# Two layers on one core: five x tiles, a bias, a transpose and the expert counts change places

## The chip, the cores and the metric

The kernel runs on one core of one Trainium2 chip. The metric is the device time of one execution in microseconds, as the median of several runs; the runs of the kernel before spread from 1205.78 to 1206.19 us. Beside it there is one profiled execution, whose time line names every instruction of every engine: TensorE (PE), VectorE (DVE), ScalarE (ACT), GpSimd (POOL) and SyncE (SP), which here only issues DMAs.

## The reference, cut to what matters

The input x is 4 images of 16 x 16 positions with 1024 channels: 1024 rows (tokens) of 1024 numbers, all in float32.

```python
x = x + conv_attention(group_norm(x))            # layer 0
t = to_tokens(x)                                  # 4 batches of 256 tokens
t = t + attention(layer_norm(t))                  # layer 1: 16 heads, causal, then
                                                  #   y @ W_proj.T + b_proj
t = t + experts(layer_norm(t))                    # gate, threshold 0.1, 8 experts
```

The experts' part, which the counts belong to:

```python
gate_logits = softmax(x @ gate_w + gate_b)
selected = gate_logits >= 0.1
weights = gate_logits * selected / (their sum)
out = sum over e of weights[:, e] * (x @ expert_w[e] + expert_b[e])
```

## The kernel before

Rows are worked on in 8 tiles of 128; tile t = 2 b + i is half i of batch b. Large products are done by a seven-product scheme (Strassen's form): a product of 2 x 2 blocks takes seven block products and some sums of blocks on VectorE. `sums_of_A` makes the sums of the row blocks s1, s2, s4 and changes a21 in place.

**End of layer 0.** Each tile of x is finished, normalised for layer 1, given the output bias b_proj by GpSimd, and stored in memory as `x_rows`. For the last two tiles worked on (tiles 4 and 6) the bias isn't added there: they are stored without it.

**Attention.** The loop over d (0 to 17) is a pipeline over 16 double steps and a lag of 2. Each step makes query and key products (`project_qk`), scores (`scores`, line 842), exponentials on ScalarE, the division by the row sums on GpSimd (`scored`, L883), a way through memory that cuts the scores in quarters (one store L889 and four loads L893 for each half, all on SP), a transpose on VectorE (`turn_back`, which calls `turned`, L898) and the product with v (`values`, pa, L911). TensorE's `values_and_scores(d)` needs the transposes of `turn_back(d)`.

From d = 13 on the output projection begins between these steps. It adds to tiles of x that `load_x` brings back from `x_rows` (GpSimd's queue, L1053), into memory that the attention's sums have left. `project_out` does a tile half directly; `product_out(b, n, ...)` does product n of the seven for the pair of tiles 2b and 2b + 1 (matmuls L980, VectorE's additions L987 to L1000). `sum_of_weights(1..4)` (L952) makes the sums of the weight blocks, 128 x 2048 each. `row_sums_out(b)` makes the row sums of pair b. Pair 1 (tiles 2 and 3) is done in d = 15 to 17 and one product more behind the loop; pair 2 (tiles 4 and 5) and then tiles 6 and 7 follow in the part called the rest here. At d = 17 GpSimd adds the bias to tiles 4 and 6 (L1103), with a tile `bp` that is loaded at d = 15 (L1084).

**The rest: projection beside the gate.** While TensorE does the remaining projection, one finished tile after another goes through eight stages: 0 normalise (statistics L1258, root L141 to L143, row on ScalarE L170, through memory in quarters as L1276 and L182; the tile itself goes to the output, L1283), 1 turn the row (L187), 2 gate sums (`parts`, L1325), 3 gate (`pg`), 4 thresholds, 5 place (the products `pp`, L1382 and L1383, with the running counts `kept`, L1380), 6 entries and 7 lists. Stages 2 to 5 take tiles 0 to 2 together, then 3 to 5, then 6, then 7.

The order is written by hand. TensorE's matmuls of this part are counted (a chunk is one matmul of 128 x 128 by 128 x 512, 0.86 us in two passes), and the table `at_chunk` says behind which chunk which (stage, tile) is put; `others` does the same for single steps, among them `row_sums_out(2)` at chunk 12. Chunks 9 to 12 are the last product of pair 1, 13 to 40 the seven of pair 2 in the order 1, 2, 6, 7, 5, 3, 4, then 8 for each half of tiles 6 and 7. Parts of the program inside `manual_schedule` keep the written order on each engine; between two such parts, and for steps outside them (the gate's constants, say, L1206 to L1245), the framework's scheduler merges by the order of the text and by what is ready, so steps of the rest can stand ahead of the loop's last ones.

The rest's tiles come from pools that lie where the attention's tiles were; a tile there waits for the last reader of what it covers. Product banks: three called mm and three called tr; pair 2's products all take mm banks in turn, so a product waits until VectorE has taken up the one three before it.

**After it.** Eight experts follow, each with its gathered rows and products; that is the larger part of the second half.

Of the kernel before, what the change touches and what calls it, by code (L numbers as in the profile page):

```python
# [32 lines left out]
F32 = mybir.dt.float32  # L33
# [6 lines left out]
P = 128  # L40
C = 1024
# [4 lines left out]
NT = TOK // P  # L46
# [16 lines left out]
Q = 4  # L63
# [6 lines left out]
def kernel(  # L70
# [27 lines left out]
    nc = tc.nc  # L98

    def pool(stack, name, bufs=1, **kw):  # L100
        return stack.enter_context(tc.tile_pool(name=name, bufs=bufs, reuse_waits="tile", **kw))
# [121 lines left out]
            nc.scalar.copy(dst[:, 4 * j : 4 * j + 4, ts(t, P)], pt.rearrange("p (c n) -> p c n", c=4))  # L223


    in_order, bp_home = ExitStack(), ExitStack()
    with ExitStack() as layer0:
        l0 = pool(layer0, "l0")
        xn = x_pool.tile([P, NC, TOK], F32, tag="x", name="xn")
# [434 lines left out]
    with ExitStack() as attention:  # L664
# [295 lines left out]
        def row_sums_out(b):  # L960
            a, s = rows_out_of(b)
            sums_of_A(*a, *s)
# [64 lines left out]
        with tc.manual_schedule():  # L1027
            for d in range(len(doubles) + lag):
                if d % 4 == 0 and d < 12:
                    load_qk(d // 4 + 1)  # L1030
                elif d == 12:
                    w_p.append(w_tile("w_p0", W_projT[:, :HALF]))

                def values_and_scores(at):
                    if at >= lag:
                        values(at - lag, turned_s.pop(at - lag))
                    if at < len(doubles):
                        made[at] = scores(at)

                def go_on(at, between=lambda: None):  # L1040
                    if at - 1 in made:
                        first_one, second_one = made.pop(at - 1)
                        soft[at - 1] = [scored(*first_one)]
                        between()
                        soft[at - 1].append(scored(*second_one))

                def turn_back(at):
                    if at >= lag:
                        turned_s[at - lag] = [turned(*one) for one in soft.pop(at - lag)]

                def load_x(*some):
                    for t in some:
                        nc.gpsimd.dma_start(xs[t], x_rows[ts(t, P), :])  # L1053

                ahead = units.get(d, ())
                if d < 14:
                    for unit in ahead[:1]:
                        project_qk(*unit)
                    turn_back(d)
                    go_on(d)  # L1060
                    for unit in ahead[1:]:
                        project_qk(*unit)
                    if d == 13:
                        sums.close()
                        x_pool = pool(x_home, "xb", side="right")
                        xs = [x_pool.tile([P, C], F32, tag=f"x{t}", name=f"xb{t}") for t in range(NT)]
                        bp = pool(bp_home, "bp", side="right").tile([P, C], F32, tag="bp", name="bp")
                        load_x(0)
                    values_and_scores(d)
                elif d == 14:  # L1070
                    project_qk(*ahead[0])
                    go_on(14, lambda: load_x(1))
                    project_qk(*ahead[1])
                    turn_back(14)
                    w_p.append(w_tile("w_p1", W_projT[:, HALF:]))
                    sums_out.append(big_tile(1, "sums_out", (4 * Q, HALF)))
                    load_x(2)
                    project_out(*outs[14][0], {NC - 3: lambda: values_and_scores(14)}, True)
                    turn_back(15)
                    project_out(*outs[14][1], {}, True)  # L1080
                    go_on(15)
                    load_x(3)
                elif d == 15:
                    nc.gpsimd.dma_start(bp, b_proj.partition_broadcast(P))  # L1084
                    product_out(1, 1, tr)
                    product_out(1, 2, tr, {1: lambda: values_and_scores(15)})
                    sum_of_weights(1)
                    sum_of_weights(2)
                    project_out(*outs[15], {NC - 1: lambda: go_on(16)}, True)
                    row_sums_out(1)  # L1090
                    load_x(4, 6)
                    turn_back(16)
                elif d == 16:
                    project_out(*outs[16], {}, True)
                    load_x(5, 7)
                    product_out(1, 6, mm)
                    sum_of_weights(3)
                    product_out(1, 5, mm, {1: lambda: values_and_scores(16)})
                    sum_of_weights(4)
                    turn_back(17)  # L1100
                else:
                    for b, nt in tiles[NT - 2 :]:
                        nc.gpsimd.tensor_add(xs[2 * b + nt], xs[2 * b + nt], bp)  # L1103
                    product_out(1, 3, tr)
                    product_out(1, 7, tr, {1: lambda: values_and_scores(17)})
        share_banks("ps_rest", 3)
        bp_home.close()


    left.close()  # L1110
# [91 lines left out]
    with ExitStack() as gating:  # L1202
# [149 lines left out]
            nc.scalar.activation(weight, weight, AF.Exp)  # L1352
            return weight, top, keep

        def thresholds(weight, top, keep):
            n = top.shape[1]
            all_of = top.unsqueeze(2).to_broadcast([P, n, E])
            if n > 1:
                nc.vector.tensor_reduce(top, weight, AX.X, ALU.add)
            nc.vector.reciprocal(top, top)  # L1360
            if n == 1:
                of = weight[:, 0, :]
                nc.vector.tensor_scalar(keep[:, 0, :], of, top, THRESHOLD, ALU.mult, ALU.is_ge)
                nc.vector.scalar_tensor_tensor(of, of, top, keep[:, 0, :], ALU.mult, ALU.mult)
            else:
                nc.vector.tensor_mul(weight, weight, all_of)
                nc.vector.tensor_scalar(keep, weight, THRESHOLD, None, ALU.is_ge)
                nc.vector.tensor_mul(weight, weight, keep)
            nc.vector.tensor_reduce(top, weight, AX.X, ALU.add)
            nc.vector.scalar_tensor_tensor(top, top, 0.0, top, ALU.is_equal, ALU.add)  # L1370
            nc.vector.reciprocal(top, top)
            nc.vector.tensor_mul(weight, weight, all_of)
            return keep

        def place(tiles, keep):


            n, t0 = len(tiles), tiles[0]
            for i, t in enumerate(tiles):
                nc.vector.tensor_add(kept[:, t + 1, :], kept[:, t, :], keep[:, i, :])  # L1380
            pp = tr(f"pp{t0}")[:, : n * E]
            nc.tensor.matmul(pp, before, keep.rearrange("p n e -> p (n e)"), start=True, stop=False)  # L1382
            nc.tensor.matmul(  # L1383
                pp, ones, kept[:, t0 : t0 + n, :].rearrange("p n e -> p (n e)"), start=False, stop=True
            )
            slot = of_tiles("place", n, E)
            nc.vector.scalar_tensor_tensor(slot, keep, 0.0, from_end[:, t0 : t0 + n, :], ALU.is_equal, ALU.mult)
            at = l2w.tile([P, 3, n, E], I32, tag="at", name=f"at{t0}", padded_shape=[P, 3, 3, E])
            nc.vector.tensor_add(at[:, 0, :, :], slot, pp.rearrange("p (n e) -> p n e", n=n))
            nc.vector.tensor_scalar(at[:, 1, :, :], at[:, 0, :, :], 31, None, ALU.bitwise_and)  # L1390
            nc.vector.tensor_scalar(at[:, 2, :, :], at[:, 0, :, :], 5, None, ALU.logical_shift_right)
            return at
# [74 lines left out]
        def stage(n, t):  # L1467
            tiles = together[t]
            if n == 0:
                normal[t] = normalise(t)  # L1470
            elif n == 1:
                turned_rows[t] = turn_rows(t, normal[t])
            elif n == 2:
                summed[t] = gate_sums(tiles)
            elif n == 3:
                gated[t] = gate(tiles, summed[t])
            elif n == 4:
                gated[t] = thresholds(*gated[t])
            elif n == 5:
                placed[t] = place(tiles, gated[t])  # L1480
            elif n == 6:
                entered[t] = entries_of(t, t - tiles[0], placed[tiles[0]])
            else:
                enter(t, *entered[t])
# [16 lines left out]
            47: ((7, 1),),  # L1501
            48: ((1, 4),),
            50: ((7, 2),),
            53: ((1, 5),),
            55: ((2, 3),),
            57: ((0, 6),),
            58: ((3, 3),),
            59: ((4, 3),),
# [11 lines left out]
        def load_table(function):  # L1520

            of = small.tile([P, 1], F32, tag="first", name="first", bufs=1)
            nc.scalar.activation(of, ident[:, 0:1], function)

        others = {
            12: lambda: row_sums_out(2),
            29: lambda: nc.gpsimd.dma_start(
                w_p[1][:, : NC // 2, :], W_projT[:HALF, HALF:].rearrange("(c p) n -> p c n", p=P)
            ),
# [447 lines left out]
```

## Time and profile before

| | us |
|---|---|
| median of 3 runs | 1206.02 |
| lowest, highest | 1205.78, 1206.19 |
| the profiled execution | 1204.73 |
| its span, first to last instruction | 1202.9 |
| TensorE busy in the span | 1191.1 (99%) |
| VectorE busy | 799.0 (66%) |
| GpSimd busy | 416.2 (35%) |
| ScalarE busy | 211.2 (18%) |

Times in the views are microseconds from the span's start. A line of a timeline has start, length, engine, line of the program, operation, written tile <- read tiles, shape and count; in brackets stands how long the engine had been idle before it and what ended that. The granted clock of TensorE was 1.00 in all stages looked at here. In the time line, d = 15 runs from about 609 us, d = 17 from 641.7 us, chunk 9 of the rest from 652.2 us, pair 2 from 655.7 us, and the experts from about 740 us.

### The profile page before, as it was taken

The page shows a single profiled execution, that of the slowest core. Times are in us where ns is not written, and L with a number is a line of the kernel's source. Part 1 is how long each engine was busy: PE and PEld are TensorE (multiplying, and loading weights), DVE is VectorE, ACT ScalarE, POOL GpSimd, SP SyncE. Part 2 cuts the span into 40 slices and gives each one's busy share as a digit, 9 for nine tenths or more (in the row PEclk, how much of TensorE's full clock was granted, in tenths as well). Part 3 has the DMA queues.
Part 4 walks back from the last instruction along what each step waited for, and adds up shares of the span by engine and source line. Part 5 has one row for each costly group of instructions (what it writes and reads, how often), then busy time and mean ns, then how long its engine had stood idle before and what let it go on. Part 6 is the DMA issues. An engine that isn't in the chain of part 4 may idle for free.

```text
span 1202.9 us, 13637 instructions
## 1 busy us (share of the span) xinstructions
PE 1191.1 (99%) x4866; PEld 649.3 (54%) x4866; DVE 799.0 (66%) x1394; ACT 211.2 (18%) x523; POOL 416.2 (35%) x470
## 2 busy tenths in 40 slices
PE   9999999999999999999999999999999999999998
PEld 5444884788884444444544464454344435444544
DVE  5796736678332666566679867897677767667852
ACT  3310111130001222122221212111111111111111
POOL 1051351365000122222333116546474554555411
PEclk9999999999999999999999999999999999999999
DMA  9102014882201353535565777484757475666434
GB/s 348 35 1 70 19 41 112 273 277 69 70 9 62 102 174 109 163 93 167 164 199 181 228 245 242 101 234 113 223 121 220 100 241 130 189 145 198 77 62 72
DMA packets 94330, 170.83 MB, mean 142 GB/s; under 512 B 12048, under 2 KB 49440, under 8 KB 94256
## 3 DMA queue, kind: packets, MB, share of 16 engines
q1 hardware_dynamic: 72880, 105.08, 26.6%
q0 software_dynamic: 16960, 54.59, 19.1%
q10 hardware_dynamic: 4416, 10.22, 2.4%
q8 instruction: 40, 0.66, 0.2%
q14 instruction: 34, 0.28, 0.1%
HBM read 117.17 MB, written 48.50 MB: 138 GB/s over the span
## 4 chain that ended last, share of the span: by engine, by line
PE 93%; DVE 3%; DMA 2%; issue 1%; SPq 0%; ACT 0%; POOL 0%; DVEq 0%; POOLq 0%
PE p L1662 27%; PE pqk L682 15%; PE pv L682 8%; PE joint L1724 4%; PE pq_pair L413 4%; PE pq L328 4%; PE left L1769 3%; PE po L1006 3%; PE pT L525 3%; PE py L617 2%; PE pk L444 2%; PE pc L465 2%; PE pv L553 2%; PE sc L842 2%; PE rest L1783 2%; PE pa L911 2%
## 5 line engine op out<-in xcount | busy, mean ns | idle before, releaser
L1145 POOL DMA_INDIRECT w_e_xg<-rows,gather x146 | 164.3, 1125 | 54.2 <-issue 42.4
L1662 PE MATMUL p<-w_e,A 128*128 128x512 f32 x368 | 162.1, 593 | 0.0
L883 POOL TENSOR_TENSOR s_q<-s_q,total 128x128 f32<-128x128 f32 (+1 forms) x128 | 61.8, 518 | 275.3 <-DVE total L880 264.4
L1662 PEld LDWEIGHTS p<-w_e,A 128*128 128x128 f32 x368 | 69.6, 190 | 86.8 <-issue 85.9
L1168 POOL DMA_INDIRECT out_dram<-y,add x32 | 58.7, 1834 | 163.6 <-issue 78.6
L1662 PE MATMUL p<-T,S 128*128 128x512 f32 x256 | 112.7, 592 | 0.0
L1711 ACT ACTIVATE y<-y,slot 128x512 f32<-128x512 f32 x64 | 45.4, 721 | 318.1 <-DVE y L1676 146.6
L682 PE MATMUL pqk<-ln,w_qk 128*128 128x512 f32 x192 | 85.7, 595 | 0.0
L1662 PEld LDWEIGHTS p<-T,S 128*128 128x128 f32 x256 | 48.6, 190 | 60.8 <-issue 60.3
L868 ACT ACTIVATE s_q<-sc,top 128x128 f32<-128x128 f32 (+1 forms) x128 | 52.0, 419 | 156.4 <-DVE top L864 137.8
L682 PEld LDWEIGHTS pqk<-ln,w_qk 128*128 128x128 f32 x192 | 36.1, 190 | 43.7 <-issue 42.1
L682 PE MATMUL pqk<-T,S_qk 128*128 128x512 f32 x128 | 57.8, 595 | 0.0
L1662 PE MATMUL p<-w_e,S 128*128 128x512 f32 x128 | 57.5, 592 | 0.0
L1006 PE MATMUL po<-w_p,y_T 128*128 128x512 f32 x112 | 50.7, 599 | 0.0
L328 PE MATMUL pq<-w_q,xn 128*128 128x512 f32 x96 | 44.5, 599 | 0.3 <-ACT xn L308 0.3
L682 PE MATMUL pv<-w_v,ln 128*128 128x256 f32 x192 | 43.2, 379 | 0.0
L1769 PE MATMUL left<-w_e,one 128*32 128x512 f32 x312 | 41.8, 593 | 0.0
L1662 PEld LDWEIGHTS p<-w_e,S 128*128 128x128 f32 x128 | 24.3, 190 | 30.6 <-issue 28.9
L898 DVE STREAM_TRANSPOSE s_T<-s_rows 128x768 f32<-128x768 f32 x32 | 30.2, 962 | 15.9 <-DMA s_rows<-s_rows 15.7
L187 DVE STREAM_TRANSPOSE A<-w_e_xg 128x1024 f32<-128x1024 f32 x32 | 39.5, 1235 | 1.4 <-DMA w_e_xg<-rows,gather 1.3
L682 PEld LDWEIGHTS pqk<-T,S_qk 128*128 128x128 f32 x128 | 24.0, 190 | 29.2 <-issue 27.7
L682 PEld LDWEIGHTS pv<-w_v,ln 128*128 128x128 f32 x192 | 36.4, 190 | 4.9
(388 smaller groups left out, 2056.0 us busy)
## 6 DMA issues: line engine op xcount, KB each, us to landing
w_e<-in_expert_w_dram SPq DMA_DIRECT2D x13, 2048.0 KB, 11.4
s_rows<-s_q SPq DMA_DIRECT2D x32, 384.0 KB, 2.3
s_rows<-s_rows SPq DMA_DIRECT2D x128, 96.0 KB, 2.4
w_qk<-in_W_attnT_dram SPq DMA_DIRECT2D x8, 1024.0 KB, 5.7
w_e<-in_expert_w_dram ACTq DMA_DIRECT2D x3, 2048.0 KB, 11.2
w_q<-in_Wq_dram SPq DMA_DIRECT2D x16, 256.0 KB, 6.8
x_at<-in_x_dram POOLq DMA_DIRECT2D x8, 512.0 KB
w_p<-in_W_projT_dram SPq DMA_DIRECT2D x2, 2048.0 KB, 8.3
```

Source lines behind the costliest of these rows:

```text
L328: nc.tensor.matmul(pq, xn[:, c, ts(t, P)], w_q[kc][:, c, :], start=(c == 0), stop=(c == NC - 1))
L413: nc.tensor.matmul(bank, a[:, c, :], b[:, c, :], start=(c == 0), stop=(c == NC // 2 - 1))
L682: nc.tensor.matmul(bank, stationary(c), moving(c), start=(c == 0), stop=(c == NC // 2 - 1))
L868: nc.scalar.activation(blocks(h, qt), psc[:, h, cols].rearrange("p (b f i) -> p b f i", f=Q, i=32), AF.Exp, bias=top[:, qt, h : h + 1], sc ...
L883: nc.gpsimd.tensor_mul(blocks(h, qt), blocks(h, qt), total[:, qt, h : h + 1].unsqueeze(2).unsqueeze(3).to_broadcast([P, 1 + qt, Q, 32]),)
L1006: nc.tensor.matmul(po, y_T[:, c, ts(t, P)], w_p[j][:, c, :], start=(c == 0), stop=(c == NC - 1))
L1145: nc.gpsimd.indirect_dma_start(out=row[:, g, :], out_offset=None, in_=table[: (TOK - P) * Q, :] if e in SHORT else table, in_offset=bass.I ...
L1168: nc.gpsimd.indirect_dma_start(out=out[: TOK - P, :] if e in SHORT else out, out_offset=bass.IndirectOffsetOnAxis(ap=add[:slots, e, k : k ...
L1662: nc.tensor.matmul(bank, a[:, c, :], b[:, c, :], start=(c == 0), stop=(c == NC // 2 - 1))
L1711: nc.scalar.mul(y, y, slot[:, e, 1, k : k + 1])
L1724: nc.tensor.matmul(of, a[:, c, :], b[:, c, :], start=(c == 0), stop=(c == NC // 4 - 1))
L1769: nc.tensor.matmul(bank[ts(i, 32), :], stationary, w[of][j][:, c, :], start=(c == 0), stop=(c == NC - 1))
```

## The change

- The tile `bp` isn't a pool of its own any more and isn't loaded at d = 15. It is made ahead of the rest in the pool l2w, under the tag that the experts' bias uses later, and loaded there on GpSimd's queue.
- Tiles 4 and 6 get their bias (`add_bias`, GpSimd) at chunks 13 and 22 of the rest and no longer at d = 17.
- x tile 4 is loaded at the end of d = 14 with tile 3; tiles 5, 6 and 7 are loaded at d = 17 on SP's queue. Before, 4 and 6 were loaded at d = 15 and 5 and 7 at d = 16, on GpSimd's queue.
- `turn_back(17)` stands ahead of `sum_of_weights(4)`.
- The additions to `kept` move from stage 5 (place) to stage 4 (thresholds), each behind its tile's selection.
- The turn of tile 5 moves from chunk 53 to 54, the gate sums of tiles 3 to 5 from 55 to 56.
- `row_sums_out(2)` moves from chunk 12, behind tile 2's normalisation, to chunk 10, ahead of it.

```diff
@@ -223,7 +223,7 @@
             nc.scalar.copy(dst[:, 4 * j : 4 * j + 4, ts(t, P)], pt.rearrange("p (c n) -> p c n", c=4))
 
 
-    in_order, bp_home = ExitStack(), ExitStack()
+    in_order = ExitStack()
     with ExitStack() as layer0:
         l0 = pool(layer0, "l0")
         xn = x_pool.tile([P, NC, TOK], F32, tag="x", name="xn")
@@ -1064,7 +1064,6 @@
                         sums.close()
                         x_pool = pool(x_home, "xb", side="right")
                         xs = [x_pool.tile([P, C], F32, tag=f"x{t}", name=f"xb{t}") for t in range(NT)]
-                        bp = pool(bp_home, "bp", side="right").tile([P, C], F32, tag="bp", name="bp")
                         load_x(0)
                     values_and_scores(d)
                 elif d == 14:
@@ -1079,32 +1078,28 @@
                     turn_back(15)
                     project_out(*outs[14][1], {}, True)
                     go_on(15)
-                    load_x(3)
+                    load_x(3, 4)
                 elif d == 15:
-                    nc.gpsimd.dma_start(bp, b_proj.partition_broadcast(P))
                     product_out(1, 1, tr)
                     product_out(1, 2, tr, {1: lambda: values_and_scores(15)})
                     sum_of_weights(1)
                     sum_of_weights(2)
                     project_out(*outs[15], {NC - 1: lambda: go_on(16)}, True)
                     row_sums_out(1)
-                    load_x(4, 6)
                     turn_back(16)
                 elif d == 16:
                     project_out(*outs[16], {}, True)
-                    load_x(5, 7)
                     product_out(1, 6, mm)
                     sum_of_weights(3)
                     product_out(1, 5, mm, {1: lambda: values_and_scores(16)})
+                    turn_back(17)
                     sum_of_weights(4)
-                    turn_back(17)
                 else:
-                    for b, nt in tiles[NT - 2 :]:
-                        nc.gpsimd.tensor_add(xs[2 * b + nt], xs[2 * b + nt], bp)
+                    for t in (5, 6, 7):
+                        nc.sync.dma_start(xs[t], x_rows[ts(t, P), :])
                     product_out(1, 3, tr)
                     product_out(1, 7, tr, {1: lambda: values_and_scores(17)})
         share_banks("ps_rest", 3)
-        bp_home.close()
 
 
     left.close()
@@ -1352,8 +1347,8 @@
             nc.scalar.activation(weight, weight, AF.Exp)
             return weight, top, keep
 
-        def thresholds(weight, top, keep):
-            n = top.shape[1]
+        def thresholds(tiles, weight, top, keep):
+            n = len(tiles)
             all_of = top.unsqueeze(2).to_broadcast([P, n, E])
             if n > 1:
                 nc.vector.tensor_reduce(top, weight, AX.X, ALU.add)
@@ -1361,10 +1356,13 @@
             if n == 1:
                 of = weight[:, 0, :]
                 nc.vector.tensor_scalar(keep[:, 0, :], of, top, THRESHOLD, ALU.mult, ALU.is_ge)
+                nc.vector.tensor_add(kept[:, tiles[0] + 1, :], kept[:, tiles[0], :], keep[:, 0, :])
                 nc.vector.scalar_tensor_tensor(of, of, top, keep[:, 0, :], ALU.mult, ALU.mult)
             else:
                 nc.vector.tensor_mul(weight, weight, all_of)
                 nc.vector.tensor_scalar(keep, weight, THRESHOLD, None, ALU.is_ge)
+                for i, t in enumerate(tiles):
+                    nc.vector.tensor_add(kept[:, t + 1, :], kept[:, t, :], keep[:, i, :])
                 nc.vector.tensor_mul(weight, weight, keep)
             nc.vector.tensor_reduce(top, weight, AX.X, ALU.add)
             nc.vector.scalar_tensor_tensor(top, top, 0.0, top, ALU.is_equal, ALU.add)
@@ -1376,8 +1374,6 @@
 
 
             n, t0 = len(tiles), tiles[0]
-            for i, t in enumerate(tiles):
-                nc.vector.tensor_add(kept[:, t + 1, :], kept[:, t, :], keep[:, i, :])
             pp = tr(f"pp{t0}")[:, : n * E]
             nc.tensor.matmul(pp, before, keep.rearrange("p n e -> p (n e)"), start=True, stop=False)
             nc.tensor.matmul(
@@ -1475,7 +1471,7 @@
             elif n == 3:
                 gated[t] = gate(tiles, summed[t])
             elif n == 4:
-                gated[t] = thresholds(*gated[t])
+                gated[t] = thresholds(tiles, *gated[t])
             elif n == 5:
                 placed[t] = place(tiles, gated[t])
             elif n == 6:
@@ -1501,8 +1497,8 @@
             47: ((7, 1),),
             48: ((1, 4),),
             50: ((7, 2),),
-            53: ((1, 5),),
-            55: ((2, 3),),
+            54: ((1, 5),),
+            56: ((2, 3),),
             57: ((0, 6),),
             58: ((3, 3),),
             59: ((4, 3),),
@@ -1522,8 +1518,16 @@
             of = small.tile([P, 1], F32, tag="first", name="first", bufs=1)
             nc.scalar.activation(of, ident[:, 0:1], function)
 
+        bp = l2w.tile([P, Q, C // Q], F32, tag="bias", name="bp", bufs=1).rearrange("p a b -> p (a b)")
+        nc.gpsimd.dma_start(bp, b_proj.partition_broadcast(P))
+
+        def add_bias(t):
+            nc.gpsimd.tensor_add(xs[t], xs[t], bp)
+
         others = {
-            12: lambda: row_sums_out(2),
+            10: lambda: row_sums_out(2),
+            13: lambda: add_bias(4),
+            22: lambda: add_bias(6),
             29: lambda: nc.gpsimd.dma_start(
                 w_p[1][:, : NC // 2, :], W_projT[:HALF, HALF:].rearrange("(c p) n -> p c n", p=P)
             ),
```

## The prediction

> **What bounds the kernel now.** I read the page first: busy times and the chain of waits.
>
> ```profile
> PE 1191.1 (99%) x4866; PEld 649.3 (54%) x4866; DVE 799.0 (66%) x1394; ACT 211.2 (18%) x523; POOL 416.2 (35%) x470
> PE 93%; DVE 3%; DMA 2%; issue 1%; SPq 0%; ACT 0%; POOL 0%; DVEq 0%; POOLq 0%
> ```
>
> TensorE is the bound. The change neither adds nor removes a product, so it can only move TensorE's idle time: 1202.9 - 1191.1 = 11.8 us in the whole span. Everything the diff touches runs between about 585 and 735 us. So the next view is TensorE's waits in 590 to 740 us (what waited, for what, us, times, longest):
>
> ```profile
> PE pa L911 <- DVE s_T L898: 2.1, 2, 1.8
> PE pp L1383 <- DVE kept L1380: 1.0, 1, 1.0
> PE row_pt L1303 <- DVE row L1282: 0.5, 1, 0.5
> PE po L980 <- DVE xb L996: 0.2, 1, 0.2
> ```
>
> TensorE's timeline gives the places (start, length, idle time and releaser in brackets):
>
> ```profile
> 648.85 1.64 PE L911 MATMUL pa<-s_T,v 128*64 128x256 f32 x16 [1.85 <-DVE s_T L898]
> 662.92 3.70 PE L980 MATMUL po<-sums_out 128*128 128x512 f32 x8 [0.21 <-DVE xb L996]
> 683.79 0.40 PE L1383 MATMUL pp<-kept,ones 128*128 128x24 f32 x2 [0.98 <-DVE kept L1380]
> ```
>
> The edits aim at these three. Together they are 1.85 + 0.21 + 0.98 = 3.04 us, the most that can be won. A difference under 0.2% (2.4 us) is about what a measurement of this kernel cannot tell from no change, so even the full prize is only just visible.
>
> **Who makes TensorE late.** VectorE's timeline ahead of the first gap, then GpSimd's:
>
> ```profile
> 637.54 1.74 DVE L991 TENSOR_TENSOR xb<-xb,sums_out 128x512 f32<-128x512 f32 x1
> 639.20 4.43 DVE L952 TENSOR_TENSOR w_p<-w_p 128x2048 f32<-128x2048 f32 x1
> ...
> 645.54 2.28 DVE L952 TENSOR_TENSOR sums_out<-w_p,sums_out 128x2048 f32<-128x2048 f32 x1
> 647.74 1.82 DVE L898 STREAM_TRANSPOSE s_T<-s_rows 128x768 f32<-128x768 f32 x2
> ```
>
> ```profile
> 631.68 2.16 POOL L1053 DMA_DIRECT2D xb<-x_rows  x4
> 636.38 5.10 POOL L1103 TENSOR_TENSOR xb<-xb,bp 128x1024 f32<-128x1024 f32 x2 [2.55 <-DMA xb<-x_rows]
> ```
>
> The transposes that TensorE waits for (turn_back(17)) stand behind the fourth weight sum, 2.28 us. The third sum took 4.43 us where its like takes 2.28, and L991 took 1.74 where a 128x512 add takes 0.69: both ran while GpSimd added the bias (636.38 to 641.48). And the chain of waits shows that the scores' second half came late through memory anyway:
>
> ```profile
> 634.05 8.85 DMA s_rows<-s_q
> ...
> 644.28 2.49 DMA s_rows<-s_rows
> ```
>
> The first took 8.85 us, where the median of its line is 2.3, with the four x loads of 631.68 in flight. The second landed at 646.8, so at 647.0, when TensorE was ready, only the first transpose could have been done.
>
> **The change, part by part.**
>
> *turn_back(17) before the fourth sum.* VectorE is free for it at 645.54 or sooner. Even if the DMAs stayed as late as now, the first transpose ends at 646.5, the second (landing 646.8 + 0.97) at 647.8. The first eight products need only the first, so at most 0.1 us of the 1.85 remains. The fourth sum then ends by 650.1 at the latest; its user (L980 of the last product of pair 1) starts at 650.4 in the moved schedule. Gain 1.85.
>
> *The x tiles.* Tile 4 takes the place that the bias load had on GpSimd's queue (614.8), same size. Tiles 5, 6 and 7 go on SP behind the scores' five DMAs, so those find the DMA engines free at 634: 2.3 to 3.6 us for 8.85, landing near 641. This is cover for the first gain, worth nothing more by itself. Three more issues on SP (0.38 each) stand ahead of SP's later stores and quarter loads, which before began at 654.98. First use of these tiles is near 670, so nobody waits. [...]
>
> *The two bias additions.* Removing them at 636.38 gives VectorE back (1.74 - 0.69) + (4.43 - 2.28) = 3.2 us, all of it before 643.6, where TensorE did not wait. They come back on GpSimd behind the load of the bias. That tile is now the first of its pool, so I expect it where the last-read values v lie: its load waits for the last pa (near 648.5 now), behind the gate's fill, two loads and constants (2.5 us, as from 650.57 to 653.07 before), so issue near 651.5 and, by the 4.1 us that the first of the four x loads took (632.2 to 636.3), landing near 655. Adds from 655 to 660, 2.34 us each. First users: L989 on tile 4, which TensorE needs (its bank) at 664.4; tile 6 is used near 690. Slack 4 us and more.
>
> What they can hurt is VectorE at 655 to 660. The rows: an add of two operands in SBUF stretched by 1.05 and 2.15 us, while L987 at 636.81, with one operand in PSUM, kept its 0.69. Cost between 0 and, from these rows, 3.2 us (4.7 if VectorE stands still for both adds) on VectorE. [...]
>
> *Side effect of that tile.* If it is the pool's first, the first normalised row no longer lies over v. Before, ScalarE's first row stood idle for 18.12 us until the last pa (650.54), with its inputs ready at 634.3. It may now run at once, and with it the second row's root and its two small VectorE instructions. That takes about 0.3 us off VectorE after 650 and moves 3 MB of stores and loads into 636 to 650. I cost it at nothing; if it crowds the scores' DMAs, see the rival.
>
> *Row sums at chunk 10.* Same four instructions, 0.69 each = 2.8 us, now ahead of tile 2's normalisation, not behind it. Both stand before L996, which frees the bank that TensorE waited for at 662.92. So the order does not take work from before L996. It helps if the sums run in VectorE's idle time before the last pa; the scheduler already pulled tile 0's and 1's statistics forward like this (627.98, 634.25).
>
> *Counts with the thresholds.* Three adds, 0.53 us together, move from 683.40 to 678.5, so the second pp product finds them done: gain 0.98. Their new place delays the thresholds by 0.53, ahead of no waiting TensorE. The turn of tile 5 and the next gate sums move one chunk (0.86) later against TensorE, which comes 0.98 sooner there, while VectorE's chain is 0.5 shorter: even. Cost 0.
>
> **Where VectorE gives back.** With the first gap closed TensorE reaches the product of 662.92 at 662.71 - 1.85 = 660.86. VectorE must have ended L996. Before, from L998 at 649.50 to L996's end at 662.87 was 13.4 us with 0.9 idle. Now L998 starts near 647.3 (transposes 643.2 to 645.0, fourth sum to 647.3). The same work without the idle ends at 647.3 + 12.5 = 659.8, plus the collision: 0 to 4.7. If the row sums are pulled ahead of the constants, the adds meet about one two-operand instruction (L994), 1 to 2 us: end 660.8 to 661.8, wait 0 to 0.9. I take 0.4, near the low end, because L996 itself has an operand in PSUM.
>
> Sum: 3.04 - 0.4 = 2.6 us. The profiled execution took 1204.73 us (span 1202.9 and 1.8 around it), so 1202.1 by it; it was 1.3 below the median of the runs, and from the median 1206.02 - 2.6 = **1203.4**.
>
> **Rivals.**
> 1. *VectorE takes the gap over* (no change, chance 0.36): the sums are not pulled forward and meet the adds. L996 then ends at 662 to 663 and TensorE waits 1.1 to 2.1 at the same product; only 0.98 and a rest remain, 1203.6 to 1206. For it: VectorE was 5.34 of 6 us busy in 655 to 661. Against: the scheduler's pulling forward.
> 2. *Slower* (0.17): the same collision at its full 4.7 us. L996 ends at 664.5, TensorE waits 3.6; and tile 2's normalisation, now behind the sums, ends 4 us later than at 659.61. Its row goes through memory (ACT row 659.65, transpose 670.65) and TensorE needs it within the gate sums, 1.0 us after 671.70. Its transpose would end near 676 for a need at 672.7, so net 3.04 - 0.2 - 3.3 - 2 = 2.5 us lost: 1208.5. It decides from about 3 us of collision on.
> 3. *The edits do not do what they say* (within the 0.36): SP's queue puts tile 0's stores and quarter loads ahead of the scores' last four DMAs, and these land at 649, not 646.8. Then 1.85 shrinks to nothing and 1205 remains.
>
> **Chances.** Forecast, the gaps closed and at most 0.6 us given back (1202.9 to 1203.6): 0.47, all of it faster by over 0.2%. Rivals 1 and 3, 0.36: within 0.2%. Rival 2, 0.17. The range runs from the full prize, 1203.0, with the 0.4 by which such runs differ, to the point where rival 2 begins to count: 1202.6 to 1207.3. The forecast alone: 1202.8 to 1203.7.
>
> **What would show it.** Right: no idle time before pa near 647; s_rows<-s_q near 3 us; L952's third sum at 2.3 us; pp without a wait; GpSimd's two adds near 655. Wrong: a wait of over 0.6 us on L996 or L989 at the sixth product of the second pair; row sums of 1.5 us and more each; the gate sums waiting for a transpose; pa still waiting for s_T. Outside 590 to 735 us nothing should differ.

## The result and the profile after

The changed kernel took 1210.34 us (median of 6 runs, 1209.05 to 1211.3), the kernel before 1205.68 (6 runs, 1204.89 to 1206.19): ratio 1.0038, 95% interval 1.0025 to 1.0051. It is slower, by about 4.7 us, and lies above the predicted range. The profiled execution took 1209.66 us with a span of 1207.9; before it was 1204.73 and 1202.9.

The page's busy times: TensorE still does the same 4866 matmuls; its busy time is 0.8 us more (1191.1 before) and the span 5.0.

```profile
span 1207.9 us, 13640 instructions
PE 1191.9 (99%) x4866; PEld 648.9 (54%) x4866; DVE 799.1 (66%) x1394; ACT 211.3 (17%) x523; POOL 416.0 (34%) x467
```

TensorE's waits between 590 and 745 us (what waited, for what, us in total, times, longest):

```profile
PE po L980 <- DVE xb L996: 5.1, 1, 5.1
PE parts L1320 <- DVE row_T L187: 0.9, 1, 0.9
PE row_pt L1298 <- DVE row L1277: 0.6, 1, 0.6
PE pa L911 <- DVE s_T L898: 0.4, 1, 0.4
```

The 0.4 on pa is an earlier one, at 598.42 us. The last pa near 647 and pp no longer wait. TensorE's timeline shows the same places as before:

```profile
646.93 1.52 PE L911 MATMUL pa<-s_T,v 128*64 128x256 f32 x16
...
665.76 5.09 PE L980 MATMUL po<-sums_out 128*128 128x512 f32 x8 [5.10 <-DVE xb L996]
...
677.90 0.65 PE L1320 MATMUL parts<-row_T,gw 128*32 128x128 f32 x16 [0.88 <-DVE row_T L187]
...
687.99 0.38 PE L1379 MATMUL pp<-kept,ones 128*128 128x24 f32 x2
```

Two gaps are closed, but the third, the sixth product of pair 2, has grown from 0.21 to 5.10 us. There is something else in its line: its eight passes took 5.09 us where they took 3.70 before. The table of windows shows why. Its columns are the window, its length, busy time of PE, PEld, DVE, ACT and POOL (instructions in brackets), then TensorE's granted clock, the DMA share and GB/s:

```profile
663.00:665.70 2.70, 0.00 (x0) 0.00 (x0) 2.33 (x8) 0.76 (x2) 0.00 (x0) 0.91 0.34 121
665.70:668.50 2.80, 2.73 (x4) 1.19 (x5) 2.19 (x4) 1.27 (x2) 0.00 (x0) 0.50 0.95 290
668.50:669.50 1.00, 1.00 (x4) 0.52 (x3) 0.96 (x3) 0.00 (x0) 0.00 (x0) 0.95 1.06 434
```

At the end of the long idle time the clock fell to half and stayed there for some 3 us of work. Around the 1.85 us gap of before it had stayed at 1.00.

VectorE's timeline tells who was late:

```profile
637.54 0.69 DVE L991 TENSOR_TENSOR xb<-xb,sums_out 128x512 f32<-128x512 f32 x1
638.15 2.28 DVE L952 TENSOR_TENSOR w_p<-w_p 128x2048 f32<-128x2048 f32 x1
...
643.10 1.83 DVE L898 STREAM_TRANSPOSE s_T<-s_rows 128x768 f32<-128x768 f32 x2
...
648.50 0.88 DVE L929 TENSOR_SCALAR y_T<-pa,bv 128x256 f32<-128x256 f32 x2 [0.81 <-PE pa L911]
650.41 0.69 DVE L987 TENSOR_TENSOR sums_out<-po,sums_out 128x512 f32<-128x512 f32 x1 [1.03 <-PE po L980]
...
654.56 5.06 DVE L1230 COPY copies<-ident 32x128 f32<-32x128 f32 x4
...
660.12 0.69 DVE L160 TENSOR_TENSOR sums_out<-y_T 128x512 f32<-128x512 f32 x1
...
665.03 0.68 DVE L996 TENSOR_TENSOR xb<-xb,po 128x512 f32<-128x512 f32 x1
```

The third weight sum and L991 are back at their plain lengths, as forecast. But four tiny copies of the gate's constants (L1230, the loop that fills `copies`) took 5.06 us. In GpSimd's timeline the two bias additions stand at the same time, and the chain of waits (start, length, what) takes the four copies apart: two of over 2 us, then, with the additions over, two of 0.22.

```profile
654.42 4.65 POOL L1525 TENSOR_TENSOR xb<-xb,bp 128x1024 f32<-128x1024 f32 x2 [2.92 <-DMA bp<-in_b_proj_dram]
```

```profile
654.64 2.20 DVE copies L1230
...
656.86 2.29 DVE copies L1230
...
659.16 0.22 DVE copies L1230
```

**Where the 4.3 us come from.** From 609 us, where the two traces coincide, to the experts' first products: -1.85 (pa) + 4.89 (L996's wait, 0.21 to 5.10) + 1.39 (half clock, 3.70 to 5.09) + 0.88 (gate sums) - 0.98 (pp) = +4.33. The experts begin 4.29 us later and the last line of products as much (1183.08 to 1187.37). The rest of the span's 5.0 arises behind it.

**The theory** to be tested: VectorE's copies (0.22 us alone, 2.20 and 2.29 here) and its sums of two operands from SBUF (L991 and L952 before, 1.74 and 4.43 us beside the additions, 0.69 and 2.28 here) stand still while a GpSimd addition runs. The change moved those additions from a stretch where TensorE did not wait to one where VectorE was already the last to come. The rival: VectorE is simply overfull before L996, by the row sums pulled ahead or by the transposes taken before the fourth sum, and the additions matter little.

### The profile page after: what moved, and what is told of

Its sections match the earlier page's. It is cut to its first block, busy times and chain, and to the rows that moved or that the text cites. A ratio compares the mean times of both kernels' runs of the same rounds, so it can differ in the third digit from the quotient of the medians.

```text
span 1207.9 us, 13640 instructions
## 1 busy us (share of the span) xinstructions
PE 1191.9 (99%) x4866; PEld 648.9 (54%) x4866; DVE 799.1 (66%) x1394; ACT 211.3 (17%) x523; POOL 416.0 (34%) x467
## 4 chain that ended last, share of the span: by engine, by line
PE 95%; DVE 2%; DMA 1%; SPq 0%; issue 0%; ACT 0%; DVEq 0%
PE p L1666 27%; PE pqk L682 16%; PE pv L682 8%; PE joint L1728 4%; PE pq_pair L413 4%; PE po L1006 4%; PE pq L328 3%; PE left L1773 3%; PE pT L525 3%; PE po L980 2%; PE py L617 2%; PE pk L444 2%; PE pc L465 2%; PE pv L553 2%; PE sc L842 2%; PE pa L911 2%
```

## The experiments

Twelve kernels, in three groups, each group on one chip beside the kernel before, whose medians there were 1204.84, 1204.84 and 1204.58 us; so ratios are compared. "From the change" and "from before" name the kernel that was edited.

### no_adds: the change without the additions

```diff
-            13: lambda: add_bias(4),
-            22: lambda: add_bias(6),
```

> The changed kernel without the two bias additions of chunks 13 and 22 (tiles 4 and 6 then lack the output bias; the bias is still loaded). Theory A (the additions on GpSimd, 654.4 to 659.1, hold VectorE's two copies of 2.2 us each, and these make L996 late): the copies at L1230 take 0.22 us each, L996 ends near 661.6, TensorE waits about 1.0 us at the sixth product of pair 2 and keeps its full clock there. Tile 2's row still goes to memory later than before the change, since the row sums stand ahead of it, so the gate sums wait for its transpose by up to 2 us. Time 1204.5 to 1206. Rival B (the row sums' place alone makes L996 late): the wait stays at 4 us or more, time above 1208.5. Rival C (tile 0's early loads and the x tiles on SP crowd something): no change, 1210.

1206.3 us, ratio 1.0006 (0.9997 to 1.0015). VectorE's copies, then TensorE:

```profile
655.09 0.89 DVE L1230 COPY copies<-ident 32x128 f32<-32x128 f32 x4
```

```profile
662.13 3.70 PE L980 MATMUL po<-sums_out 128*128 128x512 f32 x8 [0.93 <-DVE xb L996]
...
674.09 1.05 PE L1320 MATMUL parts<-row_T,gw 128*32 128x128 f32 x16 [2.10 <-DVE row_T L187]
675.07 3.22 PE L980 MATMUL po<-sums_out 128*128 128x512 f32 x4
```

The copies fall by 4.17 us (5.06 to 0.89) and the wait for L996 by the same 4.17 (5.10 to 0.93): at this product the additions act through these copies alone. But the gain does not come up: with TensorE no longer late, a second wait of 2.10 us appears at the gate sums, and after it the next products run slowly again (four passes in 3.22 us, 1.98 elsewhere). Theory A named that wait but not its slow clock, and the time is 0.3 us above the expected 1206.

### adds_in_loop and adds_loop_sums12: the additions at another time

Both from the change: bias and x tiles 4 and 6 are loaded at the end of d = 14, GpSimd adds at the head of d = 17. The second also puts the row sums back to chunk 12.

```diff
-                    load_x(3, 4)
+                    load_x(3, 4, 6)
+                    nc.gpsimd.dma_start(bp, b_proj.partition_broadcast(P))
...
-                    for t in (5, 6, 7):
+                    for t in (4, 6):
+                        nc.gpsimd.tensor_add(xs[t], xs[t], bp)
+                    for t in (5, 7):
...
# the second only
-            10: lambda: row_sums_out(2),
+            12: lambda: row_sums_out(2),
```

> The changed kernel with the bias part as it was in place, but earlier: bias and x tiles 4 and 6 loaded on GpSimd at the end of d = 14, the additions on GpSimd at the head of d = 17, so right behind the last divisions of the scores (from about 632 us); tiles 5 and 7 stay on SP. Theory A: the additions run from 632 to 637, where VectorE had idle time, the copies at L1230 take 0.22 us each, and the rest is as without additions: 1204.5 to 1206. Rival B: as the changed kernel, above 1208.5. Rival C: 1209 or more.

> As the kernel before it in this list, and row_sums_out(2) back at chunk 12, behind tile 2's normalisation. Theory A with the row sums as a second, smaller cost (tile 2's row 2.8 us later through memory): the wait at the sixth product stays near 1 us, no wait at the gate sums, and the gains of the other edits show: 1203 to 1204. If the row sums' place costs nothing, the same time as with them at chunk 10. Rival B: this one alone is fast, and by 4 us or more against the kernel with the sums at chunk 10.

adds_in_loop: 1206.5 us, ratio 1.0015 (1.0007 to 1.0024). adds_loop_sums12: 1202.63 us, ratio 0.9989 (0.998 to 0.9999), below the changed kernel and just below the kernel before; three of its twelve executions took 1205.4 to 1207.3, and no trace shows why. In adds_in_loop GpSimd adds from 630.70 to 635.81, a stretch where VectorE is not the last to come; the collision is there (a 128x1 instruction took 2.06 us) and TensorE does not feel it:

```profile
633.77 2.06 DVE L169 SCALAR_TENSOR_TENSOR ln_less<-ln_mv,ln_rstd 128x1 f32<-128x1 f32 x1
```

What remains of its loss is at the gate sums, in TensorE's timeline:

```profile
673.33 0.64 PE L1325 MATMUL parts<-row_T,gw 128*32 128x128 f32 x16 [2.19 <-DVE row_T L187]
673.90 3.65 PE L980 MATMUL po<-sums_out 128*128 128x512 f32 x4
```

With the row sums at chunk 12 this wait is gone, and so is the slow product behind it; the wait for L996 is the same (0.94, against 0.92):

```profile
661.50 3.70 PE L980 MATMUL po<-sums_out 128*128 128x512 f32 x8 [0.94 <-DVE xb L996]
...
670.28 1.52 PE L1325 MATMUL parts<-row_T,gw 128*32 128x128 f32 x48
671.72 1.98 PE L980 MATMUL po<-sums_out 128*128 128x512 f32 x4
```

The pair therefore prices the row sums' move: 2.19 of waiting and 3.65 - 1.98 = 1.67 of slow clock (granted 0.50 from 674 to 677), 3.86 us; the medians differ by 3.87, an agreement closer than medians with intervals of about 1 us to each side can vouch for. The move lets 2.8 us of VectorE work stand ahead of tile 2's statistics, and that tile's row goes through memory and back before TensorE's gate sums need it.

### counts_only and turn_only: single parts on the kernel before

counts_only takes the three edits of the counts (additions in `thresholds`, chunks 54 and 56) and nothing else. turn_only takes the exchange alone:

```diff
+                    turn_back(17)
                     sum_of_weights(4)
-                    turn_back(17)
```

> The kernel before with the counts' edit alone: additions to kept in the thresholds, turn of tile 5 at chunk 54, gate sums of tiles 3 to 5 at chunk 56. If the prediction's third term was right: no wait ahead of the second pp product, 1.0 us less, about 1204.7. If the moved chunks or the longer thresholds cost something: 1205.7 or more.

> The kernel before with one edit, the last transposes of the scores ahead of the fourth weight sum. Theory (VectorE is the bound after that point): the wait before pa falls from 1.85 us to at most 0.3, and the 6th product of pair 2 waits 1 to 2 us for L996 in its place (0.2 before), since VectorE's work up to L996 is the same; time within 1 us of the kernel before, 1204 to 1205. Rival (the gap is won for good): both waits gone, 1.8 us less, 1203.

counts_only: 1203.64 us, ratio 0.9987 (0.9979 to 0.9996). The wait of pp is gone; the waits of pa (1.62) and L996 (0.22) stay. The 0.98 us of the prediction is there. turn_only: 1203.74 us, ratio 0.9991 (0.9982 to 1.0), with these waits of TensorE:

```profile
PE po L980 <- DVE xb L996: 1.4, 1, 1.4
PE pp L1383 <- DVE kept L1380: 1.0, 1, 1.0
PE row_pt L1303 <- DVE row L1282: 0.5, 1, 0.5
PE pa L911 <- DVE s_T L898: 0.3, 1, 0.3
```

The 0.3 on pa is an earlier one, at 598.69 us (0.21 in the kernel before). The gap of 1.85 ahead of the last pa is gone, and 1.2 us of it come back as a wait for L996: VectorE's work up to L996 is what it was. So by these waits the exchange gains about 0.6 us by itself, too little for this comparison to show.

### sums12: the row sums back, the additions where the change put them

```diff
-            10: lambda: row_sums_out(2),
+            12: lambda: row_sums_out(2),
```

> The changed kernel with row_sums_out(2) back at chunk 12 and the bias additions left where the change put them. Theory A (two separate costs: the additions' collision with the copies, some 4.1 us on VectorE, and the row sums ahead of tile 2's row): the copies at L1230 still take 2.2 us twice, TensorE still waits some 5 us at the sixth product of pair 2 and runs at half its clock for some 3 us after that, but the gate sums do not wait for the transpose: 0.9 to 1.5 us less than the changed kernel, that is about 4 us more than before, 1.003 to 1.0035 of it. Rival B (the sums' place is the main cost): at or below the time of before.

1208.67 us, ratio 1.0036 (1.0025 to 1.0047): no gain that can be told from the change. The gate sums no longer wait, but the sixth product starts as late as with the change, and the half clock lasts longer:

```profile
665.61 5.71 PE L980 MATMUL po<-sums_out 128*128 128x512 f32 x8 [5.13 <-DVE xb L996]
```

0.88 won, 5.71 - 5.09 = 0.62 lost. In the changed kernel the 5.10 us wait had already made TensorE late enough to hide most of what the row sums cost.

### warm_fill: the long wait filled with idle products

From the change: 17 products of 128 x 128, whose result nobody reads, ahead of the sixth product of pair 2.

```diff
+                if (b, n) == (2, 6):
+                    fill = tr("fill")
+                    for _ in range(17):
+                        nc.tensor.matmul(fill[:, :P], before, ones, start=True, stop=True)
```

> The changed kernel with 17 idle products of 128 x 128 (about 4.4 us, their result is used by nothing) ahead of the sixth product of pair 2, where TensorE waits 5.1 us. If the slow first products after the wait (5.09 us for eight where 3.70 is usual) come from the idle time itself: the clock stays at 1.00 and 1.4 us come back, 1.0027 of before against 1.0038 to 1.004. If they come from a transfer or from VectorE's traffic: no change.

1208.8 us, ratio 1.0041 (1.0026 to 1.0056). TensorE:

```profile
660.50 3.96 PE L1557 MATMUL fill<-ones,before 128*128 128x128 f32 x34
665.83 3.70 PE L980 MATMUL po<-sums_out 128*128 128x512 f32 x8 [1.37 <-DVE xb L996]
...
677.55 0.64 PE L1320 MATMUL parts<-row_T,gw 128*32 128x128 f32 x16 [1.86 <-DVE row_T L187]
```

The product starts at the same time (665.83, before 665.76) and takes 3.70 instead of 5.09: the slow product was the clock, not the data. But the gate sums now wait 1.86 us instead of 0.88, so 1.0 of the 1.4 us goes to the next wait; the profiled span is 0.9 us shorter, and the comparison does not show it.

### early_constants and best: the gate's constants at another time

Both put the gate's constants (`quarters`, `copies` and others) into memory that is free from the end of layer 0; early_constants from the change, best from adds_loop_sums12.

```diff
+    early = pool(ctx, "early")
     with ExitStack() as attention:
...
-        copies = l2.tile([P, Q, Q, 32], F32, tag="copies", name="copies")
+        copies = early.tile([P, Q, Q, 32], F32, tag="copies", name="copies")
```

> The changed kernel with the gate's constants (copies, quarters, token, from_end, quarter, ones) in a pool under the attention's, so that the scheduler sets them earlier; 3.7 us of VectorE's work leave the stretch ahead of L996. The additions stay at 654 to 659 and now meet row sums or L994, at most one or two of them. Theory A: L996 ends by 660, no wait at the sixth product of pair 2; the gate sums wait at most 1 us for tile 2's transpose: 2 to 3 us below before, 0.9975 to 0.9985. If the additions hold VectorE whatever it runs: 4 us lost again, 1.001 or more.

> Bias additions at the head of d = 17, row sums at chunk 12, constants early: nothing of the three costs left. TensorE waits neither at pa, nor at the sixth product, nor at the gate sums, nor at the second pp product: the full 3.0 us below before, 0.9975. If there is a fourth cost that the wait at the sixth product hid: 0.9985 or more, and the waits name it.

early_constants: 1213.47 us, ratio 1.0069 (1.005 to 1.0088). best: 1210.88 us, ratio 1.0046 (1.003 to 1.0062). Both missed. After 600 us no wait for L996 is left in either, as was meant; in early_constants the gate sums still wait 1.91 us for tile 2's transpose, where at most 1 was expected, and the four passes behind them take 3.33 us (1.98 elsewhere). But the scheduler took the constants at the first moment at which they could run, the end of layer 0, and there GpSimd has four 128x1024 additions of its own (259.58 to 269.09, 2.35 each). VectorE in early_constants:

```profile
262.43 2.13 DVE L1207 COPY quarters<-ident 32x8 f32<-32x8 f32 x2
...
264.84 4.29 DVE L1207 COPY quarters<-ident 32x8 f32<-32x8 f32 x2
```

Four copies of 32x8, 0.16 us each elsewhere, took 6.4 us, TensorE waited 4.89 us at 272.15 (5.13 in best), and its clock was at 0.50 until 277.7. In the chain of waits these copies stand ahead of the root, the row on ScalarE and the products that waited; a few products later, at 282.7, TensorE has lost 7.9 us against the kernel before (7.3 in best). It is the same loss at another place, with other GpSimd work and smaller copies.

### scalar_copies, sums12_scalar and best_scalar: the copies on ScalarE

The same edit on the change, on sums12 and on adds_loop_sums12:

```diff
-            nc.vector.tensor_copy(
+            nc.scalar.copy(
                 copies[ts(g, 32), g, :, :], ident[ts(g, 32), ts(g, 32)].unsqueeze(1).to_broadcast([32, Q, 32])
```

> The changed kernel with the four copies of the identity's blocks (32x128 each) moved from VectorE to ScalarE; everything else stays, so that GpSimd's two additions of 654.4 to 659.1 us meet what VectorE does next: the reciprocal and the small instructions of tile 1, then tile 2's four row sums, which read two operands from SBUF. Theory (any VectorE instruction of the kinds that were stretched is held up until an addition ends): the copies no longer cost 5.06 us of VectorE, but the first row sums now take over 1 us each instead of 0.69 and end at the earliest near 660.5; L996 ends near 662.5 to 663.5, the 6th product of pair 2 waits 2 to 3.5 us (5.1 before the edit), and the gate sums wait for tile 2's row as without the additions (2.1): 1207 to 1209 us. Rival (only the copies are sensitive): row sums at 0.69 us each, wait on L996 at most 1, gate sums 2.1: near 1206, like the kernel without the additions.

> The changed kernel with the row sums back at chunk 12 and the same four copies on ScalarE; the additions stay where the change put them. Theory (what costs is which VectorE instruction stands beside the additions): beside them now stand tile 1's small instructions and tile 2's statistics, which read one operand; the row sums come after 658. L996 ends near 661 to 662.5, the wait before the 6th product is 0.9 to 2 us, no idle time of 5 us and no half clock, no wait at the gate sums: 1202.5 to 1204 us. Rival (the additions hold up VectorE whatever it does, 4.7 us in all): L996 near 665, wait about 4 us: 1207 to 1208.

> The kernel with the additions in the attention's loop and the row sums at chunk 12 (1202.6 us), with the four copies on ScalarE. There TensorE waited 0.94 us for L996 and VectorE was busy without a break from 650.3 to 661.4; the copies are 0.89 us of that. Theory (VectorE's plain amount of work is what is left before the 6th product): the wait falls to 0 to 0.2 us and the time to about 1201.8. Rival (the copies are not on that path, or ScalarE's row of tile 1 comes later for them): no change, 1202.6.

**scalar_copies**: 1208.64 us, ratio 1.003 (1.002 to 1.004). The copies take 1.22 us on ScalarE, beside the additions. What comes next on VectorE is hit instead, the row sums, which read two operands from SBUF:

```profile
654.90 0.69 DVE L160 TENSOR_TENSOR sums_out<-y_T 128x512 f32<-128x512 f32 x1
655.62 2.73 DVE L161 TENSOR_TENSOR sums_out<-sums_out,y_T 128x512 f32<-128x512 f32 x1
658.39 2.72 DVE L162 TENSOR_TENSOR sums_out<-y_T,sums_out 128x512 f32<-128x512 f32 x1
661.03 0.68 DVE L163 TENSOR_TENSOR y_T<-y_T 128x512 f32<-128x512 f32 x1
```

2.73 + 2.72 - 2 x 0.69 = 4.07 us lost, against 4.17 on the copies. GpSimd is held up too: L160 began at 654.90, the first addition at 654.92, and the two additions take 5.64 us where they take 4.65 with the change. The sixth product waits 3.97 us and starts 1.14 us sooner than with the change, but takes 6.47 us at half clock; the product after it starts at 670.92, with the change at 670.69. The expected end of the row sums (660.5) and wait (2 to 3.5) were too low, and the clock was not in that expectation at all; the time lies in the expected 1207 to 1209.

**sums12_scalar**: 1204.74 us, ratio 1.0005 (0.9996 to 1.0014). Here the additions (654.55 to 659.22) meet tile 1's last small instruction and tile 2's statistics:

```profile
654.70 2.22 DVE L169 SCALAR_TENSOR_TENSOR ln_less<-ln_mv,ln_rstd 128x1 f32<-128x1 f32 x1
656.84 1.27 DVE L1253 BATCH_NORM_STATS2 ln_stats<-xb 128x6 f32<-128x512 f32 x2
```

A 128x1 instruction with two operands in SBUF stood 2.2 us; the statistics, with one operand of 128x512, ran beside the second addition at their plain length (1.27 us for two, 1.28 in sums12 with no addition beside them). So two additions of 4.67 us cost VectorE 2.06, and the wait for L996 is 2.05 us, at full clock. The expected wait (0.9 to 2) and product length held. No wait at the gate sums was expected; at the first of them there is none, at the second, at 699.77, there are 0.61 us. The time is 0.7 us above the expected 1204.

**best_scalar**: 1203.31 us, ratio 0.9986 (0.9977 to 0.9995), the same as adds_loop_sums12 within the intervals. The wait for L996 fell from 0.94 to 0.64 only, and the expected 1201.8 was missed: the root of tile 2 stands behind the copies and tile 1's row on ScalarE, and VectorE idles 1.01 us for it (0.29 without the edit). And the second gate sums, near 699.6, now wait 0.60 us for a turn (no wait without the edit). The copies leave VectorE, but their time is not won. None of these combinations is clearly faster than the counts' edit alone (0.9987): of what the exchange saves ahead of the last pa a part is given back at L996, and the rest is too little for these comparisons.

## Why the prediction was wrong

**What held.** The gap before pa closed (1.85). The counts brought 0.98. The scores' way through memory is quicker: `s_rows<-s_q`, 8.85 us before, is now, in the list of DMA issues between 630 and 640 us (KB, us to landing):

```profile
s_rows<-s_q SPq DMA_DIRECT2D x1, 384.0 KB, 2.9
```

The third weight sum went to 2.28 us. GpSimd's additions stand at 654.42 to 659.07, forecast 655 to 660; the bias load was issued at 650.61, forecast 651.5. The three x loads on SP and the first row, now at 634, cost nothing visible.

**The step that failed: what stands beside the additions.** The prediction bounded the collision by 0 to 4.7 us, and measured is 4.17: the bounds were right. The value taken, 1 to 2 us of which TensorE would feel at most 0.9, rested on "if the row sums are pulled ahead of the constants, the adds meet about one two-operand instruction (L994)". In the trace after, L994 was over at 652.6, the row sums came at 660.12 behind the constants, and the additions met the four copies. The prediction had looked only at additions with two operands as things that can be hit; it had shown no row of a copy beside a GpSimd addition, in either direction, so nothing excluded them. The rows of the runs show them hit: copies of 0.22 took 2.20 and 2.29 (the changed kernel), two-operand sums of 0.69 took 2.73 and 2.72 (scalar_copies), one-operand statistics stayed at 1.27 (sums12_scalar). For the copies the price did not follow their size but the rest of GpSimd's addition: with the change they ended at 656.84 and 659.15, the additions at 656.77 and 659.07; in early_constants copies of 32x8 ended at 264.38, 266.83 and 269.13, the additions at 264.37, 266.80 and 269.09.

**VectorE's idle time.** The same sum let L996 end at 659.8 without a collision: 12.5 us of work without the 0.9 us of idle time. The work is 12.4 to 12.5, but no_adds and the change have 2.1 us of idle in it: 0.81 and 1.03 us for pa and po, 0.27 for a root. TensorE came sooner, but VectorE also reached these points sooner and waited for TensorE there. With 2.1 us of idle L996 ends near 661.5, TensorE waits 0.9 (0.93 in no_adds, 0.94 in adds_loop_sums12), and the forecast's 0.4 was too little even without a collision. So 0.7 of the 1.85 us came back at the next place whatever the additions did; in turn_only, where the additions and the copies don't meet either, 1.2 came back.

**Row sums at chunk 10** were costed at nothing, since both orders stand before L996. That asked only about L996. The other reader of the order is tile 2's row; it costs 3.86 us as soon as nothing else holds TensorE up. The prediction has this only inside rival 2, as a result of the collision. No run shows a gain of this edit.

**The clock** was in no term. A gap was counted as its own length, but one of 5.10 us cost 6.49.

**The rivals.** Rival 2 is the case that came: the collision nearly in full, L996 late, the gate sums waiting for tile 2's row. It put L996's end at 664.5 and the wait at 3.6; measured 665.71 and 5.10, most of the difference being the idle time above. Its 1208.5 lacks the 1.39 us of clock. Its condition, "from about 3 us of collision on", was met by the copies, not by the instructions that it named. Rival 1's place was right, its size not. Rival 3 did not happen.

## What to carry to other kernels

Before moving GpSimd work, list every VectorE instruction in the target window, by operands: here, behind GpSimd additions of about 2.35 us, copies of 0.22 us lost 2.0 and 2.1, two-operand sums of 128x512 2.0 each and a two-operand instruction of 128x1 2.06, while single-operand statistics kept their 1.27; put GpSimd's additions beside those, or where TensorE is not waiting for VectorE. Ask of every reordered step who else reads what it is moved past, not only the one wait at hand. And price an idle time of TensorE of about 2 us and more above its length: here, when the clock fell, by 1.4 to 2.9 us.

## What was not expected of the hardware

- **The clock fell after short gaps, and stayed down for about 3.4 or 6.8 us.** For the changed kernel the granted clock was read in windows of 0.1 us; for the others these are estimates from the mean clock of windows of 0.7 to 7 us, taking the clock in them as 1.00 or 0.50. It goes from 1.00 to 0.50 when TensorE has been idle for 2.4 us (sums12), 2.7 (scalar_copies), 3.7 (early_constants, the wait of 4.89) or 4.5 (the changed kernel). At the gate sums, behind idle times of 2.10 us (no_adds) and 2.19 (adds_in_loop), it falls 0.1 and 0.5 us after the products have begun again. It stays at 0.50 for 3.4 us in the changed kernel, no_adds and adds_in_loop, and for 6.8 us in sums12, scalar_copies and, at 272.15, early_constants. In two more places only the lengths of the products show it: behind the 1.91 us of early_constants 0.95 us for 0.64 and 3.33 for 1.98, behind the 5.13 us of best 1.97 for 1.04 and 8.21 for 7.07. Only the part that falls on work costs, and it costs half of its length: 2.8 us of work and 1.39 lost in the changed kernel, 4.1 and 2.01 in sums12, 5.6 and 2.77 in scalar_copies. That is why idle times of 5.10 and 5.13 us cost so different sums in the changed kernel and sums12, and why the shortest of these three, 3.97 us in scalar_copies, cost most. Idle times of 1.85 (before), 1.86 (warm_fill) and 2.05 us (sums12_scalar) left the clock at 1.00, so length alone doesn't decide near 2 us. The idle times of 1.86, 1.91, 2.10 and 2.19 us follow 1.08 us of narrow products (128*32); whether these matter for the clock was not tried.
- **A 128x1 instruction can cost 2 us** (L169, 2.06 and 2.22 us, 0.16 without an addition beside it), because its length is not what it waits for. In early_constants it began at 665.68, near the end of the first addition (664.24 to 666.58), and took 0.92.
